# Two scan slots per tile in a selective-scan kernel: a ring of three double tiles, GpSimd's product for two slots at once, B and C loaded two slots at a time

## The chip, the cores and the metric

The kernel runs on one core of one Trainium2 chip. The metric is the device time of one execution in microseconds (us). A core has TensorE (PE, matrix products), VectorE (DVE), ScalarE (ACT), GpSimd (POOL) and SyncE (SP, which here issues every DMA), and 16 DMA engines that move data between HBM and the on-chip memory SBUF. Matrix products land in PSUM. SBUF and PSUM have 128 partitions. Every engine works through its own queue in order, and an instruction that has to wait holds all that stand behind it on its queue.

## What is computed

The input x has shape (8, 512, 48, 48): 8 samples, 512 channels, L = 2304 positions. There are two layers, each with a group norm ahead and a residual sum behind:

```python
x = x + linear_attention(group_norm(x), Wq, Wkv)       # causal, 8 heads
x = x + mamba_blocks(group_norm(x), ...)               # 4 channel groups, one after another
```

The second layer cuts the channels into four groups of 128. Each group is added to the result of the one ahead and goes through a selective scan with 256 inner channels d and 16 states n:

```python
delta = softplus(dt @ Wdt.T + bdt);  A = -exp(A_log)
dA  = exp(delta[b,l,d] * A[d,n]);    dBu = (delta * xs)[b,l,d] * Bm[b,l,n]
h   = dA_t * h + dBu_t               # for t = 0 .. L-1
y_t = sum over n of h[d,n] * C_t[n]
```

Then y is gated, projected back to 128 channels, and fused with the group's input by a maximum and two weights that depend on means over all positions.

## The kernel before, in words

**Jobs and slots.** A job is one chunk of LC = 384 positions of one channel group of one sample; NC = 6 chunks make a block, 4 blocks a sample, so there are 192 jobs. Two streams (even and odd samples) take turns, block by block. A job has SLOTS = 8 slots. In a slot, NG = 2 pairs of states are scanned for one half h of the inner channels (slots 0 to 3 have h = 0, slots 4 to 7 h = 1). The partitions carry 64 channels times the two states of a pair; a tile u holds [128, NG, 2, 1 + 384] numbers, where column 0 holds the state that the chunk ahead left.

**The work of a slot.** `last_product` (line 866) takes a tile u from its ring, lets ScalarE copy the old state into column 0 (L872), and lets GpSimd write the product of B and delta*x for the last TAIL = 128 columns (L873). `product` (L884) has VectorE write the other 256 columns, with delta*x from a copy in PSUM (`inputs`, L857). `decay` (L894) has ScalarE make exp(delta*A) in a PSUM bank; four `scan` instructions (L905, VectorE) run the recurrence over u in place; `weigh` (L917, GpSimd) multiplies u by C in place; `keep` (L928) saves the last column as the state; `gather` (L933, TensorE) sums over the states into PSUM.

**The order.** It is written out by hand in `slot(k)` and issued in that order to all engines. Slot k starts with `product` of slot k+1, then `beside(2k)`, then its four scans. After the second scan come the `gather` of slot k-2, `last_product` of slot k+2 (with s == 7 its `product` too), and `beside(2k+1)`. After the fourth scan `weigh` of slot k is issued. The ring of u has 5 buffers, so `last_product` of slot k+2 takes the buffer that slot k-3 had.

**Halves and tasks.** `beside(half)` runs what is due in this half slot: attention chunks (`chunk`, with times counted in halves), statistics, the passing on of a block's result, and the steps of `prepare` for later jobs. With first = 2*start, the half at which a job's first slot starts, `prepare` makes the convolution at first-21 to first-19, then gate, steps and delta, stores delta and dx = delta*xs (L822, GpSimd) to HBM (`spread`, L789), and from first-7 on loads them back, repeated over the two states of a pair: `steps(h)` for delta (tile dr), `scaled(h)` for dx (tile dxr), two DMAs each (L800), one for each half of the partitions.

**B and C.** `rows(m, q)` (line 810) loads the rows of B (m = 0) or C (m = 1) that the slots q and q+4 use: from the HBM tile scr, two DMAs (L813), one for each 64 partitions, each with a source of [64, 768], all 64 rows the same 3072 B. B and C have 4 buffers each, one for each q, so a job's tile q takes the buffer of the job ahead. B goes out at first-6, -5, -3 and -1, C at first-2, first, +2 and +4. `scaled(1)` goes at first+1, `steps(1)` at first+3. The order of rows in scr is set by `bc_rows` on the host.

**Start and end.** `statistics(0)` borrows five buffers of the ring of u for the first sample's chunks; the sixth chunk is loaded after the first one's statistics. At the very end `pass_on` of the second stream borrows three of them.

Of the kernel before, what the change touches and what calls it, by code (L numbers as in the profile page):

```python
# [9 lines left out]
F32 = mybir.dt.float32  # L10
# [7 lines left out]
P = 128  # L18
T = 128
LC = 384  # L20
NG = 2
SLOTS = 8
TAIL = 128
BANKS = 6
DEPTH = 3
LEAD = 11
# [23 lines left out]
def attention_then_mamba_kernel(  # L50
# [12 lines left out]
    nc = tc.nc  # L63
    B, _, L = x.shape
    NS = 16
    NC = L // LC
# [160 lines left out]
    def statistics(b):  # L227

        xv = x[b].rearrange("(t p) l -> p t l", p=P)
        stats = small.tile([P, 4, NC, 6], F32, tag="stats_a", name=f"stats_a{b}", bufs=2)  # L230
        if b == 0:

            xs = []

            def load(c):
                t = mpool.tile([P, 4, 1 + LC], F32, tag="u", name=f"xs_{c}", bufs=5)[:, :, 0:LC]
                nc.sync.dma_start(out=t, in_=xv[:, :, c * LC : (c + 1) * LC])
                xs.append(t)

            for c in range(5):  # L240
                load(c)
            load_projections()
            for c in range(NC):
                for ct in range(4):
                    nc.vector.bn_stats(stats[:, ct, c, :], xs[c][:, ct, :])
                if c == 0:
                    load(5)
                    fetch(0)
        else:
            when = begins[b] + b % 2  # L250
            for i in range(4 * NC):
                yield (when - 4, 1) if b > 1 else "1", 0
                xs = piece(b, i)
                yield (when, 1) if b > 1 else "1", 0
                nc.vector.bn_stats(stats[:, i // NC, i % NC, :], xs)
                when += PERIOD
        norms[b] = yield from group_norm(stats, 4, f"a{b}", 2)
# [266 lines left out]
    class Stream:  # L524
# [55 lines left out]
        def pass_on(self):  # L580
# [49 lines left out]
            if last and self.z:  # L630

                got = [
                    mpool.tile([P, 4, 1 + LC], F32, tag="u", name=f"end_{i}", bufs=5)
                    for i in range(NC // 2)
                ]
                for c in range(NC):
                    fu, xa = (got[c // 2][:, c % 2 * 2 + i, 0:LC] for i in range(2))
                    cols = slice(c * LC, (c + 1) * LC)
                    rows = slice(old[1] * P, (old[1] + 1) * P)
                    nc.sync.dma_start(out=xa, in_=x1s[old[0]][rows, cols])  # L640
                    nc.sync.dma_start(out=fu, in_=old[3][:, cols])
                for c in range(NC):
                    fu, xa = (got[c // 2][:, c % 2 * 2 + i, 0:LC] for i in range(2))
                    cols, icols = slice(c * LC, (c + 1) * LC), slice(3 + c * LC, 3 + (c + 1) * LC)
                    for t, i in ((xi[:, icols], 0), (fu, 1)):
                        nc.vector.scalar_tensor_tensor(
                            xa, t, wt[:, i : i + 1], xa, ALU.mult, ALU.add
                        )
                    nc.sync.dma_start(out=out[old[0], rows, cols], in_=xa)
                return  # L650
# [39 lines left out]
    class Job:  # L690
# [6 lines left out]
        def prepare(self):  # L697
# [95 lines left out]

            src = scr.rearrange("(q i m f) l -> q m i (f l)", q=4, m=2, i=2)

            def pairs(t, rows):
                for i in range(2):
# [2 lines left out]
            def steps(h):  # L802
                self.dr[h] = drs[h]
                pairs(self.dr[h][:, :, 1 : 1 + LC], dsrc[h])
# [3 lines left out]
                pairs(self.dxr[h], xsrc[h])  # L808

            def rows(m, q):  # L810
                t = mpool.tile([P, NG, LC], F32, tag="BC"[m], name=f"{'BC'[m]}_{n}_{q}", bufs=4)
                for i in range(2):
                    nc.sync.dma_start(  # L813
                        out=t[i * 64 : i * 64 + 64].rearrange("p j l -> p (j l)"),
                        in_=src[q, m, i].partition_broadcast(64),
                    )
                (self.B, self.C)[m][q] = t

            dx = mpool.tile([P, 2, LC], F32, tag="dx", name=f"dx_{n}", bufs=1)
# [10 lines left out]
            yield first - 6, 0  # L830
            rows(0, 0)
            yield first - 5, 0
            rows(0, 1)
            self.prepared = True
            yield first - 3, 0
            rows(0, 2)
            yield first - 2, 0
            rows(1, 0)
            yield first - 1, 0
            rows(0, 3)  # L840
            yield first, 0
            rows(1, 1)
            yield first + 1, 0
            scaled(1)
            yield first + 2, 0
            rows(1, 2)
            yield first + 3, 0
            steps(1)
            yield first + 4, 0
            rows(1, 3)  # L850

        prepared = closed = False

        def inputs(self, h):

# [9 lines left out]

        def last_product(self, s):

            shape, cols = [P, NG, 2, TAIL], slice(LC - TAIL, LC)
            u = mpool.tile([P, NG, 2, 1 + LC], F32, tag="u", name=f"u_{self.n}_{s}", bufs=5)
            if self.c:  # L870
                h, q = s // 4, s % 4 * NG
                nc.scalar.copy(u[:, :, :, 0], self.state[:, h, q : q + NG, :])  # L872
            nc.gpsimd.tensor_tensor(  # L873
                u[:, :, :, 1 + LC - TAIL :],
                self.B[s % 4][:, :, cols].unsqueeze(2).to_broadcast(shape),
                self.dxr[s // 4][:, :, cols].unsqueeze(1).to_broadcast(shape),
                ALU.mult,
            )
            return u

        def product(self, s, u):

            shape, cols = [P, NG, 2, LC - TAIL], slice(0, LC - TAIL)
            nc.vector.tensor_mul(  # L884
                u[:, :, :, 1 : 1 + LC - TAIL],
                self.B[s % 4][:, :, cols].unsqueeze(2).to_broadcast(shape),
                self.dxp.unsqueeze(1).to_broadcast(shape),
            )

# [25 lines left out]
        def weigh(self, s, u):  # L915

            nc.gpsimd.tensor_tensor(  # L917
                u[:, :, :, 0:LC],
                u[:, :, :, 1:],
                self.C[s % 4].unsqueeze(2).to_broadcast([P, NG, 2, LC]),  # L920
                ALU.mult,
            )

# [216 lines left out]
    def prime(k):  # L1140
        job, s = at(k)
        hurry(k, lambda: job.prepared)
        primed.add(k)
        job.inputs(0)
        for r in range(2):
            us[k + r] = job.last_product(s + r)
        job.product(s, us[k])
        ahead(DEPTH)

    def slot(k):  # L1150
        job, s = at(k)
        end = k + 1 == slots or apart(k + 1)
        if not end and k + 1 not in drawn:
            j, r = at(k + 1)
            j.product(r, us[k + 1])
        before = jobs[k // SLOTS - 1] if k >= SLOTS else None
        if s == 2 and before is not None and not before.closed:
            before.gated(1)
            tasks.insert(0, Task(finale(before)))
        elif s == 6:  # L1160
            job.gated(0)
        beside(2 * k)
        for i in range(4):
            job.scan(s, i, us[k], decays.pop(0))
            if i == 0 and s in (2, 6):
                j = at(k + 2)[0] if s == 6 and k + 2 < slots and not apart(k + 2) else None
                early = j is not None and j.prepared
                if early:
                    j.inputs(0)
                job.skip(s // 4)  # L1170
            ahead(DEPTH)
            if i == 1:

                while kept:
                    kept.pop(0)()
                if len(waiting) > 1:
                    waiting.pop(0)()
                if s == 2:
                    job.inputs(1)
                elif s == 6 and not early and k + 2 < slots and not apart(k + 2):  # L1180
                    j = at(k + 2)[0]
                    if not j.prepared:
                        hurry(k + 2, lambda: j.prepared)
                    j.inputs(0)
                if not end and k + 2 < slots and not apart(k + 2):
                    j, r = at(k + 2)
                    us[k + 2] = j.last_product(r)
                    if s == 7:

                        j.product(r, us[k + 2])  # L1190
                        drawn.add(k + 2)
                beside(2 * k + 1)
        u = us[k]
        job.weigh(s, u)
        kept.append(lambda: at(k)[0].keep(s, u))
        waiting.append(lambda: at(k)[0].gather(s, us.pop(k)))
        if end:
            close(k)
            if k + 1 < slots:
                prime(k + 1)  # L1200
            else:
                hurry(slots, lambda: not tasks)
                flush()
# [101 lines left out]
```

## Time and profile before

| | |
|---|---|
| median of 3 runs | 8292.5 us (8291.23 to 8294.32) |
| the profiled execution | 8294.55 us, span in the profile 8292.4 us |
| first scan (L905) starts, last one starts | 192.9 us, 8269.5 us |
| first B load issued | 183.2 us |
| one scan (L905), 6144 of them | 935 ns |
| GpSimd: weighing L917, product L873, 1536 each | 3191 ns, 1287 ns |
| VectorE: product L884, 1536 | 1193 ns |
| ScalarE: state copy L872, 1280; copy to PSUM L857, 384 | 194 ns, 592 ns |
| B loads, us to landing, shortest, median, longest | 3.1, 4.6, 8.0 |
| C loads, the same | 3.0, 5.2, 9.6 |

In the groups below, a line has the code line, engine, operation, tiles out<-in, shape and count; then total busy time in us and the mean of one in ns; then the engine's idle time ahead of them, and who ended it. Matrix products are pipelined, so a busy TensorE is not one at its peak. An issue of a DMA is listed with its size and the time from issue to landing. Packets are the single pieces that the DMA engines move. The DMA share in a stretch is the mean busy share of the 16 engines, by packet times.

### The profile page before, as it was taken

How to read it: one execution, taken by the hardware profiler on the slowest of the kernel's cores; microseconds unless marked ns; L12 is line 12 of the kernel's file. 1: busy time of each engine (PE TensorE's matmuls, PEld its weight loads, DVE VectorE, ACT ScalarE, POOL GpSimd, SP SyncE). 2: the span in 40 equal slices, each digit the busy share in tenths (PEclk: the TensorE clock that was granted, in tenths of full speed). 3: DMA queues.
4: the chain of work that ended last, by engine and by line, in shares of the span. 5: the costliest groups of instructions: out<-in, count | busy, mean ns of one | idle time of the engine just before them, and what ended most of it. 6: DMA issues, size and time to landing. Idle time of an engine off the chain costs nothing. (4 is left out here: it accounts for less than half of the span.)

```text
span 8292.4 us, 128570 instructions
## 1 busy us (share of the span) xinstructions
PE 7748.5 (93%) x38850; PEld 3744.1 (45%) x38850; DVE 7952.3 (96%) x10534; ACT 6911.0 (83%) x14630; POOL 7759.7 (94%) x4235
## 2 busy tenths in 40 slices
PE   8999999998999999999999999999999999999975
PEld 4444444444444444444444444444444444444432
DVE  3999999999999999999999999999999999999998
ACT  3888888887888888888888888888888888888876
POOL 2999999999999999999999999999999999999998
PEclk9999999999999999999999999999999999999987
DMA  6667777766777777777777777777777777777665
GB/s 202 190 190 204 210 206 209 208 193 197 208 204 201 201 208 209 204 205 196 201 207 201 197 205 209 208 208 193 202 200 207 201 201 197 201 200 196 191 169 145
DMA packets 974440, 1654.65 MB, mean 200 GB/s; under 512 B 119337, under 2 KB 768169, under 8 KB 973618
## 3 DMA queue, kind: packets, MB, share of 16 engines
q1 hardware_dynamic: 973746, 1646.43, 72.2%
q8 instruction: 309, 5.06, 0.3%
q14 instruction: 385, 3.15, 0.1%
HBM read 1318.28 MB, written 327.68 MB: 198 GB/s over the span
## 5 line engine op out<-in xcount | busy, mean ns | idle before, releaser
L905 DVE TENSOR_TENSOR_SCAN u<-bank,u 128x385 f32<-128x385 f32 (+1 forms) x6144 | 5439.5, 935 | 132.0 <-ACT bank L894 129.5
L917 POOL TENSOR_TENSOR u<-u,C 128x1536 f32<-128x1536 f32 x1536 | 4901.4, 3191 | 344.6 <-DVE u L905 147.3
L894 ACT ACTIVATE bank<-dr,scales 128x385 f32<-128x385 f32 (+1 forms) x6144 | 3411.6, 578 | 673.8 <-DVE u L905 639.4
L933 PE MATMUL yp<-u,cst 128*64 128x384 f32 x12288 | 2371.8, 507 | 236.2 <-ACT yp L862 160.3
L873 POOL TENSOR_TENSOR u<-B,dxr 128x512 f32<-128x512 f32 x1536 | 1977.2, 1287 | 17.3 <-DMA B<-scr 15.7
L884 DVE TENSOR_TENSOR u<-B,dxp 128x1024 f32<-128x1024 f32 x1536 | 1831.7, 1193 | 8.2 <-ACT dxp L857 8.2
L302 PE MATMUL bank<-xn,wq 128*128 128x384 f32 x4608 | 1659.1, 502 | 90.9 <-POOL xn L326 47.8
L933 PEld LDWEIGHTS yp<-u,cst 128*64 128x64 f32 x12288 | 776.5, 138 | 1412.3 <-issue 997.1
L302 PEld LDWEIGHTS bank<-xn,wq 128*128 128x128 f32 x4608 | 833.2, 191 | 838.4 <-DVE u L905 124.3
L709 PE MATMUL bank<-xi,wk 128*128 128x384 f32 x3072 | 1103.5, 502 | 9.5 <-POOL xi L683 6.3
L709 PEld LDWEIGHTS bank<-xi,wk 128*128 128x128 f32 x3072 | 556.2, 191 | 553.3 <-DVE u L905 94.0
L314 ACT ACTIVATE ex<-bank,bqkv_sb 128x384 f32<-128x384 f32 x384 | 220.3, 574 | 416.2 <-PE bank L302 416.1
L894 ACT ACT_TABLE_LOAD x382 | 490.1, 1283 | 6.7
L822 POOL TENSOR_TENSOR dx<-delta,xs 128x384 f32<-128x384 f32 x384 | 387.4, 1009 | 22.2 <-ACT delta L780 22.2
L951 PE MATMUL bank<-yz,scales 128*128 128x384 f32 x768 | 305.4, 514 | 38.4 <-DVE yz L945 30.6
L769 PE MATMUL bank<-dbc,steps_w 9*128 9x384 f32 x768 | 305.5, 517 | 3.4 <-ACT dbc L761 2.4
L720 PE MATMUL bank<-xi,scales 128*128 128x384 f32 x768 | 290.0, 492 | 2.6 <-ACT xs L745 2.1
L756 PE MATMUL bank<-xs,scales 128*40 128x384 f32 x768 | 279.5, 486 | 0.0
L857 ACT COPY dxp<-dxr 128x512 f32<-128x512 f32 x384 | 227.2, 592 | 37.0 <-DMA dxr<-xscr 19.2
L500 PE MATMUL bank<-sm,v 128*64 128x128 f32 x2304 | 253.0, 298 | 0.0
L745 ACT ACT_TABLE_LOAD x192 | 246.3, 1283 | 4.9 <-PE bank L709 1.5
L780 ACT ACT_TABLE_LOAD x192 | 246.3, 1283 | 4.0 <-issue 0.6
(118 smaller groups left out, 7907.2 us busy)
## 6 DMA issues: line engine op xcount, KB each, us to landing
B<-scr SPq DMA_DIRECT2D x1536, 192.0 KB, 4.6
C<-scr SPq DMA_DIRECT2D x1536, 192.0 KB, 5.2
xn<-xn SPq DMA_DIRECT2D x192, 768.0 KB, 7.1
dr<-dscr SPq DMA_DIRECT2D x768, 192.0 KB, 3.8
dxr<-xscr SPq DMA_DIRECT2D x768, 192.0 KB, 4.8
dscr<-delta SPq DMA_DIRECT2D x192, 384.0 KB, 6.9
xscr<-dx SPq DMA_DIRECT2D x192, 384.0 KB, 2.4
xn<-in_x SPq DMA_DIRECT2D x48, 768.0 KB, 6.6
```

What stands on the lines that cost most here:

```text
L302: nc.tensor.matmul(ps, wqs[m // NC][:, kt, j * P : (j + 1) * P], xn[:, kt, :], start=(kt == 0), stop=(kt == 3),)
L709: nc.tensor.matmul(xc, wk[:, k, h * P : (h + 1) * P], xi[:, c0 + k : c0 + k + LC], start=(k == 0), stop=(k == 3),)
L720: nc.tensor.matmul(zp, w_gate[:, s, h * P : (h + 1) * P], xi[:, c0 + 3 : c0 + 3 + LC], start=True, stop=True,)
L769: nc.tensor.matmul(vp, steps_w[32:41, s, h * P : (h + 1) * P], dbc[32:41, :], start=True, stop=True)
L822: nc.gpsimd.tensor_tensor(dx[:, h, :], delta[:, h, :], xs[:, h, :], ALU.mult)
L873: nc.gpsimd.tensor_tensor(u[:, :, :, 1 + LC - TAIL :], self.B[s % 4][:, :, cols].unsqueeze(2).to_broadcast(shape), self.dxr[s // 4][:, :, ...
L884: nc.vector.tensor_mul(u[:, :, :, 1 : 1 + LC - TAIL], self.B[s % 4][:, :, cols].unsqueeze(2).to_broadcast(shape), self.dxp.unsqueeze(1).to ...
L894: nc.scalar.activation(dA[:, cols], self.dr[h][:, g, cols], AF.Exp, scale=w_a[:, self.w[1], 2 * h + g, q + j : q + j + 1],)
L905: nc.vector.tensor_tensor_scan(u[:, j, g, cols], dA[:, cols], u[:, j, g, cols], 0.0, ALU.mult, ALU.add,)
L917: nc.gpsimd.tensor_tensor(u[:, :, :, 0:LC], u[:, :, :, 1:], self.C[s % 4].unsqueeze(2).to_broadcast([P, NG, 2, LC]), ALU.mult,)
L933: nc.tensor.matmul(self.yp[g * 64 : g * 64 + 64, 0:LC], pair_sum, u[:, j, g, 0:LC], start=False, stop=(s % 4 == 3 and j == NG - 1), skip_g ...
L951: nc.tensor.matmul(self.xm[:, 0:LC], w_out[:, self.w[1], h, :], self.yz[:, h, :], start=(h == 0), stop=(h == 1),)
```

## The change

The tile u now holds two slots: [128, 4, 2, 1 + 384], in a ring of 3 (six slots in all). `last_product` is called in even slots only, for slots k+2 and k+3 together: one copy of the old states and one GpSimd product with 4 state pairs. It hands back two views of the tile, one for each slot. TAIL goes from 128 to 144, so VectorE's product has 240 columns. B and C tiles hold two slots' rows, [128, 4, 384], with 2 buffers each; `part` picks a slot's share. A tile is loaded by one DMA whose source is [2, 64, 1536]: two rows of 6144 B in HBM, each repeated for 64 partitions. B goes out at first-6 and first-4, C at first-2 and first+3; `steps(1)` goes at first+2, ahead of the second C tile. `prepared` is set at first-5. At the start all six chunks of the first sample are loaded into the three double tiles; at the end two of them are borrowed. The host orders the rows of scr to match.

```diff
@@ -20,7 +20,7 @@
 LC = 384
 NG = 2
 SLOTS = 8
-TAIL = 128
+TAIL = 144
 BANKS = 6
 DEPTH = 3
 LEAD = 11
@@ -230,21 +230,23 @@
         stats = small.tile([P, 4, NC, 6], F32, tag="stats_a", name=f"stats_a{b}", bufs=2)
         if b == 0:
 
-            xs = []
+            xs, halves = [], []
 
             def load(c):
-                t = mpool.tile([P, 4, 1 + LC], F32, tag="u", name=f"xs_{c}", bufs=5)[:, :, 0:LC]
+                if c % 2 == 0:
+                    both = mpool.tile([P, 8, 1 + LC], F32, tag="u", name=f"xs_{c}", bufs=3)
+                    halves.append(both)
+                t = halves[c // 2][:, c % 2 * 4 : c % 2 * 4 + 4, 0:LC]
                 nc.sync.dma_start(out=t, in_=xv[:, :, c * LC : (c + 1) * LC])
                 xs.append(t)
 
-            for c in range(5):
+            for c in range(NC):
                 load(c)
             load_projections()
             for c in range(NC):
                 for ct in range(4):
                     nc.vector.bn_stats(stats[:, ct, c, :], xs[c][:, ct, :])
                 if c == 0:
-                    load(5)
                     fetch(0)
         else:
             when = begins[b] + b % 2
@@ -630,9 +632,12 @@
             if last and self.z:
 
                 got = [
-                    mpool.tile([P, 4, 1 + LC], F32, tag="u", name=f"end_{i}", bufs=5)
-                    for i in range(NC // 2)
+                    mpool.tile([P, 2 * NG, 2, 1 + LC], F32, tag="u", name=f"end_{i}", bufs=3).rearrange(
+                        "p a b l -> p (a b) l"
+                    )
+                    for i in range(2)
                 ]
+                got = [got[0][:, 0:4], got[0][:, 4:8], got[1][:, 0:4]]
                 for c in range(NC):
                     fu, xa = (got[c // 2][:, c % 2 * 2 + i, 0:LC] for i in range(2))
                     cols = slice(c * LC, (c + 1) * LC)
@@ -793,7 +798,7 @@
 
 
 
-            src = scr.rearrange("(q i m f) l -> q m i (f l)", q=4, m=2, i=2)
+            src = scr.rearrange("(q i m f) l -> q m i (f l)", q=2, m=2, i=2)
 
             def pairs(t, rows):
                 for i in range(2):
@@ -808,12 +813,11 @@
                 pairs(self.dxr[h], xsrc[h])
 
             def rows(m, q):
-                t = mpool.tile([P, NG, LC], F32, tag="BC"[m], name=f"{'BC'[m]}_{n}_{q}", bufs=4)
-                for i in range(2):
-                    nc.sync.dma_start(
-                        out=t[i * 64 : i * 64 + 64].rearrange("p j l -> p (j l)"),
-                        in_=src[q, m, i].partition_broadcast(64),
-                    )
+                t = mpool.tile([P, 2 * NG, LC], F32, tag="BC"[m], name=f"{'BC'[m]}_{n}_{q}", bufs=2)
+                nc.sync.dma_start(
+                    out=t.rearrange("p j l -> p (j l)"),
+                    in_=src[q, m].unsqueeze(1).to_broadcast([2, 64, 2 * NG * LC]),
+                )
                 (self.B, self.C)[m][q] = t
 
             dx = mpool.tile([P, 2, LC], F32, tag="dx", name=f"dx_{n}", bufs=1)
@@ -830,26 +834,22 @@
             yield first - 6, 0
             rows(0, 0)
             yield first - 5, 0
+            self.prepared = True
+            yield first - 4, 0
             rows(0, 1)
-            self.prepared = True
-            yield first - 3, 0
-            rows(0, 2)
             yield first - 2, 0
             rows(1, 0)
-            yield first - 1, 0
-            rows(0, 3)
-            yield first, 0
-            rows(1, 1)
             yield first + 1, 0
             scaled(1)
             yield first + 2, 0
-            rows(1, 2)
+            steps(1)
             yield first + 3, 0
-            steps(1)
-            yield first + 4, 0
-            rows(1, 3)
+            rows(1, 1)
 
         prepared = closed = False
+
+        def part(self, tiles, s):
+            return tiles[s % 4 // 2][:, s % 2 * NG : s % 2 * NG + NG]
 
         def inputs(self, h):
 
@@ -865,25 +865,25 @@
 
         def last_product(self, s):
 
-            shape, cols = [P, NG, 2, TAIL], slice(LC - TAIL, LC)
-            u = mpool.tile([P, NG, 2, 1 + LC], F32, tag="u", name=f"u_{self.n}_{s}", bufs=5)
+            shape, cols = [P, 2 * NG, 2, TAIL], slice(LC - TAIL, LC)
+            u = mpool.tile([P, 2 * NG, 2, 1 + LC], F32, tag="u", name=f"u_{self.n}_{s}", bufs=3)
             if self.c:
                 h, q = s // 4, s % 4 * NG
-                nc.scalar.copy(u[:, :, :, 0], self.state[:, h, q : q + NG, :])
+                nc.scalar.copy(u[:, :, :, 0], self.state[:, h, q : q + 2 * NG, :])
             nc.gpsimd.tensor_tensor(
                 u[:, :, :, 1 + LC - TAIL :],
-                self.B[s % 4][:, :, cols].unsqueeze(2).to_broadcast(shape),
+                self.B[s % 4 // 2][:, :, cols].unsqueeze(2).to_broadcast(shape),
                 self.dxr[s // 4][:, :, cols].unsqueeze(1).to_broadcast(shape),
                 ALU.mult,
             )
-            return u
+            return [u[:, 0:NG], u[:, NG : 2 * NG]]
 
         def product(self, s, u):
 
             shape, cols = [P, NG, 2, LC - TAIL], slice(0, LC - TAIL)
             nc.vector.tensor_mul(
                 u[:, :, :, 1 : 1 + LC - TAIL],
-                self.B[s % 4][:, :, cols].unsqueeze(2).to_broadcast(shape),
+                self.part(self.B, s)[:, :, cols].unsqueeze(2).to_broadcast(shape),
                 self.dxp.unsqueeze(1).to_broadcast(shape),
             )
 
@@ -917,7 +917,7 @@
             nc.gpsimd.tensor_tensor(
                 u[:, :, :, 0:LC],
                 u[:, :, :, 1:],
-                self.C[s % 4].unsqueeze(2).to_broadcast([P, NG, 2, LC]),
+                self.part(self.C, s).unsqueeze(2).to_broadcast([P, NG, 2, LC]),
                 ALU.mult,
             )
 
@@ -1142,8 +1142,7 @@
         hurry(k, lambda: job.prepared)
         primed.add(k)
         job.inputs(0)
-        for r in range(2):
-            us[k + r] = job.last_product(s + r)
+        us[k], us[k + 1] = job.last_product(s)
         job.product(s, us[k])
         ahead(DEPTH)
 
@@ -1184,7 +1183,8 @@
                     j.inputs(0)
                 if not end and k + 2 < slots and not apart(k + 2):
                     j, r = at(k + 2)
-                    us[k + 2] = j.last_product(r)
+                    if s % 2 == 0:
+                        us[k + 2], us[k + 3] = j.last_product(r)
                     if s == 7:
 
                         j.product(r, us[k + 2])
@@ -1251,10 +1251,10 @@
 
     bc_rows = [
         8 + 16 * m + 2 * (q + j) + i
-        for q in range(0, 8, NG)
+        for q in range(0, 8, 2 * NG)
         for i in range(2)
         for m in range(2)
-        for j in range(NG)
+        for j in range(2 * NG)
     ]
     win = np.swapaxes(np.asarray(L1_conv_in_proj_w), 1, 2)
     packed = [
```

## The prediction

> **What bounds the kernel now.** I read the busy line first, then busy times in the stretch from the first load of B to the last scan, then groups, waits, and last the DMA lines. The busy line shows four engines near full:
>
> ```profile
> PE 7748.5 (93%) x38850; PEld 3744.1 (45%) x38850; DVE 7952.3 (96%) x10534; ACT 6911.0 (83%) x14630; POOL 7759.7 (94%) x4235
> ```
>
> By stretch (columns: us, then busy us of PE, weight loads, DVE, ACT and POOL, clock, DMA share, GB/s):
>
> ```profile
> 8.00:12.00 4.00, 0.00 (x0) 0.00 (x0) 3.67 (x9) 0.00 (x0) 0.00 (x0) 1.00 1.07 380
> 183.00:8271.00 8088.00, 7592.20 (x37930) 3649.29 (x37930) 7888.32 (x10366) 6848.94 (x14504) 7721.53 (x4174) 0.98 0.73 200
> 3000.00:3420.00 420.00, 402.86 (x2043) 195.87 (x2044) 419.17 (x558) 365.44 (x783) 404.69 (x216) 1.00 0.78 211
> ```
>
> The reader is to see that VectorE sets the pace: 419.17 of 420 us in the middle stretch. 8088 us hold 192 jobs of 8 slots, so a job takes 42.1 us and a slot 5.27. DMA is at 73 to 80%, hidden. The groups that the change touches:
>
> ```profile
> L905 DVE TENSOR_TENSOR_SCAN u<-bank,u 128x385 f32<-128x385 f32 (+1 forms) x6144 | 5439.5, 935 | 132.0 <-ACT bank L894 129.5
> L917 POOL TENSOR_TENSOR u<-u,C 128x1536 f32<-128x1536 f32 x1536 | 4901.4, 3191 | 344.6 <-DVE u L905 147.3
> L873 POOL TENSOR_TENSOR u<-B,dxr 128x512 f32<-128x512 f32 x1536 | 1977.2, 1287 | 17.3 <-DMA B<-scr 15.7
> L884 DVE TENSOR_TENSOR u<-B,dxp 128x1024 f32<-128x1024 f32 x1536 | 1831.7, 1193 | 8.2 <-ACT dxp L857 8.2
> ```
>
> And DMA (packets; the kernel's queue; issues with KB and us to landing; SyncE's longest wait):
>
> ```profile
> DMA packets 974440, 1654.65 MB, mean 200 GB/s; under 512 B 119337, under 2 KB 768169, under 8 KB 973618
> q1 hardware_dynamic: 973746, 1646.43, 72.2%
> B<-scr SPq DMA_DIRECT2D x1536, 192.0 KB, 4.6
> C<-scr SPq DMA_DIRECT2D x1536, 192.0 KB, 5.2
> ...
> steps_w<-in_wdt SPq DMA_DIRECT2D x1, 36.0 KB
> bqkv_sb<-in_bqkv SPq DMA_DIRECT2D x1, 6.0 KB, 2.8
> ```
>
> ```profile
> SPq L789 <- POOL dx L822: 1085.2, 192, 9.1
> ```
>
> B and C are 3072 issues of 192 KB, 604 of the queue's 1646 MB. GpSimd and VectorE almost never wait for them.
>
> [...] The issue list adds up to 7451; if each leaves one small packet per engine used, 7450 x 16, plus 9 for the one transfer of 9 rows (steps_w, 36 KB), plus the 128 rows of 48 B of bqkv_sb make 119,337, which is the page's count to the unit. No issue with an outermost 2 is in this trace. [...] the stretch at 8 us, with every engine full, moves 380 GB/s, 23.75 per engine. [...] the rows of 384 and 512 elements (L822 and L873, 1009 and 1287 ns) give 2.17 too, but 512 to 1536 gives 1.86.
>
> **The change part by part.**
>
> *The 16 columns off VectorE.* L884 goes from 1024 to 960 elements. From 384 elements (L945, 547 ns) to 1024 (1193) an element costs 1.01 ns: 64 x 1.01 = 65 ns, 1536 times 99 us. VectorE is the bound now, so all would count. The copy that feeds it (L857) shrinks from 512 to 480, some 12 us of ScalarE, off the path.
>
> *GpSimd's product for two slots.* 1536 of 512 elements become 768 of 1152. With 1.86 ns, 1287 + 640 x 1.86 = 2477 against 2574 for two, 75 us less in all; with 2.17, 2676, 78 us more. I take zero. Queued behind the longer instruction is the weighing L917 of the same slot: in even slots GpSimd has 2.5 to 2.7 + 3.19 us, and mostly another 1.0, in a slot of 5.27, in odd slots only 3.19 and the rest. The weighing so comes up to 1.6 us later; its reader, the gather on TensorE, is put one and a half slots (7.9 us) after the scans, which covers 3.2 + 1.6. Without this cover TensorE would wait up to 1.6 us in each of 768 pairs.
>
> *The ring.* Before, slot k+2 takes the buffer of k-3; after, the pair k+2, k+3 takes that of k-4, k-3. The last gather waited for is the same: nothing. The state copy L872 (1280 x 194 ns) becomes 640 of 8 elements, up to 124 us less of ScalarE, which has 1239 us free in the stretch: nothing.
>
> *Start and end.* All six loads of x go at once, ahead of the weights and the first xn; the last stage uses two tiles of the ring. A microsecond either way, taken as zero.
>
> *B and C tiles of two slots.* Bytes are equal, rows double to 6144 B, issues fall from 16 to 4 a job. At 0.58 us an issue SyncE is freed of 7 us a job, and is not the bound. The loads of B's second half move from 3 to 4 halves ahead of the job, after the product that last reads the old tile; C's second half goes out 3 halves into the job, now behind both dxr and dr of h=1 (two issues each, past which it is moved), needed at the end of slot 2. With 16 engines all that would be hidden: 768 KB in 2 to 3 us of movement.
>
> But the source of the one new transfer is [2, 64, 1536], outermost 2, where the two old ones were [64, 768]. [...] it runs on **2 of 16 engines**. The price, per job and for each of these two: B and C 604 MB / 192 / 2 = 1573 KB; everything else (1646 - 604 = 1042 MB, still over 16) 339 KB. At 23.75 GB/s that is 66.2 + 14.3 = 80.5 us, against a compute time of 42.1: DMA on two engines becomes the bound. Bounds of the rate: the page's mean, 1646 MB / (72.2% x 16 x 8292.4 us) = 17.19 GB/s[...] gives 111 us[...]. I take 23.75, since 14 engines will be mostly idle.
>
> *What is late next.* Each load can go only when its tile is free. When C's second half lands, GpSimd weighs slot 2 (3.19), then makes the second half of dx (1.01), which the same queue holds behind it; SyncE stands at that store (the wait shown above), stores it (2.4) and only then asks for the next job's dr, dxr and B. 6.6 us; xn and other loads already queued fill about half: 3.3 us. The rest of the chain (two weighings, the product, VectorE's scans) lies beside the next transfers of 16.6 us each. So 83.8 us a job.
>
> *Sum.* 183 us ahead of the first B, 192 x 83.8 = 16,090, 21 us after the last scan: 16,294, and 2.1 that lie outside the span (8294.55 less 8292.4): **16,300**. The profiled run is 2 us above the median shown, 8292.5, which is nothing here. The 99 us saved on VectorE vanish: VectorE will idle half of the time.
>
> **The rivals.**
> 1. *All 16 engines carry it, faster*[...]. 8292.4 - 99 + 2 = 8195, GpSimd's 7722 up to 78 more in 7989 still fitting. For it: the same bytes in larger rows[...]. It decides once the transfer gets about 4 engines: 393 KB + 339 KB, 31 us, fits in 42.1.
> 2. *Two engines at the slow rate*: rows read 64 times over by one engine move no faster than the 17.19 GB/s mean. B and C 91.5, the rest 14.3, gap 3.3: 109 us, 21,150. For it: B and C now make up much of the mean.
> 3. *16 engines, but GpSimd binds*: 78 us dearer product and weighings in bursts; its 7800 us with the 366 idle in the stretch kept: 8166 + 204 + 2, 8370. Against: a third of that idle time is waiting for the scans of VectorE, which get earlier.
>
> **How the numbers follow.** Main case 0.74, rival 1 0.12, rival 2 0.12, rival 3 0.02. The main case's own range is 14,100[...] to 19,000; I reach up to rival 2, 21,200, and leave out the fast cases. 0.2% (17 us) is about what a measurement tells from no change. Faster 0.11, same 0.02 (rival 1 where GpSimd takes back the gain), slower 0.87.
>
> **What would show it.** Small packets: 119,337 - 3072 x 16 + 768 x 2 = 71,721 with two engines, 82,473 with sixteen. B and C landing in 16 us or more; mean near 101 GB/s; GpSimd waiting before L917 for C and before the product for B, VectorE half idle; L884 near 1128 ns, the pair product 2477 to 2676. Wrong if B and C land in under 8 us, or if the queue's rate per engine on the two is far from 23.75.

## The result, and the profile after

| | before | after |
|---|---|---|
| median, us | 8293.41 (4 runs, 8291.23 to 8298.3) | 15,896.73 (4 runs, 15,892.3 to 15,898.02) |
| ratio, 95% interval | | 1.9161 (1.9137 to 1.9185) |
| span of the profiled execution, us | 8292.4 | 15,895.2 |

The forecast was 16,300. The page after, its busy line, the packets and the kernel's queue:

```profile
PE 9627.3 (61%) x38850; PEld 4459.1 (28%) x38850; DVE 7953.6 (50%) x10534; ACT 6930.6 (44%) x13990; POOL 7850.8 (49%) x3467
...
DMA packets 828456, 1653.93 MB, mean 104 GB/s; under 512 B 71721, under 2 KB 720553, under 8 KB 827698
...
q1 hardware_dynamic: 827826, 1646.24, 31.7%
```

The reader is to see three things. The busy time of VectorE (7952 before, 7954 after) and GpSimd (7760, 7851) hardly moved, so the 7600 us are idle time. The bytes are the same. And the DMA share fell to 31.7% while the kernel waits for DMA, which fits if a few of the 16 engines are full and the rest idle. The trace's packet records, each with its start and length, bear this out: after the first load of B exactly two packets are in flight for 64% of the time, and none for 1.5%; before, 16 was the commonest number (25% of the time), and none for 20%. The small packets say the same: 71,721 is, to the unit, 119,337 less 3072 x 16 plus 768 x 2.

The groups after (columns as before) show where the time stands:

```profile
L917 POOL TENSOR_TENSOR u<-u,C 128x1536 f32<-128x1536 f32 x1536 | 4864.6, 3173 | 4922.7 <-DMA C<-scr 4666.0
L905 DVE TENSOR_TENSOR_SCAN u<-bank,u 128x385 f32<-128x385 f32 (+1 forms) x6144 | 5436.0, 938 | 471.1 <-ACT bank L894 463.6
...
L884 DVE TENSOR_TENSOR u<-B,dxp 128x960 f32<-128x960 f32 x1536 | 1747.3, 1138 | 4261.9 <-DMA B<-scr 3107.6
L873 POOL TENSOR_TENSOR u<-B,dxr 128x1152 f32<-128x1152 f32 x768 | 2017.5, 2627 | 2951.9 <-DMA B<-scr 2507.1
```

GpSimd stood 4666 us for C and 2507 us for B, VectorE 3108 us for B; before, these waits were 10.7 us for C and under 65 us for B. SyncE, which issues all DMAs, was held as well. A stretch of its timeline after (start and length in us, line, transfer):

```profile
5999.85 13.85 SPq L624 DMA_DIRECT2D xb<-x  x1
...
6025.72 8.91 SPq L805 DMA_DIRECT2D dr<-dscr  x2
6034.73 0.52 SPq L817 DMA_DIRECT2D C<-scr  x1
6035.35 0.41 SPq L279 DMA_DIRECT2D xn<-xn  x1
6035.89 8.25 SPq L357 DMA_DIRECT2D before<-ksum  x2
```

In a line with x2, two issues share the length. Before, most issues took 0.3 to 0.6 us. Here a few transfers behind a load of B or C one issue lasts up to 14 us, and everything behind it on SyncE waits: the issue that follows the first one of this view starts at 6013.76 us, when the 13.85 us are over. What makes an issue last so long wasn't shown. The chain of work that ended last (shares of the span by engine, then by line) has 70% in DMA and SyncE's queue, and C leads.

```profile
DMA 60%; PE 17%; SPq 10%; POOL 6%; issue 3%; ACT 3%; DVE 1%; POOLq 0%; ACTq 0%; DVEq 0%
DMA C<-scr 36%; DMA before<-ksum 9%; DMA dxr<-xscr 8%; PE yp L933 5%; PE bank L714 5%; POOL u L917 4%; SPq L624 3%; DMA xo<-x 3%; SPq L357 3%; DMA xb<-x 2%; SPq L805 1%; SPq L817 1%; PE bank L304 1%; PE bank L725 1%; SPq L178 1%
```

The chain of before could be followed back over only a quarter of the span. In that part DMA has 1%, and VectorE's scans lead with 4%:

```profile
PE 8%; ACT 7%; DVE 6%; DMA 1%; POOL 1%; issue 1%; SPq 1%; POOLq 0%; ACTq 0%; DVEq 0%
```

### The profile page after: what moved, and what is told of

Read it like the earlier page. It is cut to its first block, busy times and chain, and to the rows that moved or that the text cites. A ratio compares the mean times of both kernels' runs of the same rounds, so it can differ in the third digit from the quotient of the medians.

```text
span 15895.2 us, 120224 instructions
## 1 busy us (share of the span) xinstructions
PE 9627.3 (61%) x38850; PEld 4459.1 (28%) x38850; DVE 7953.6 (50%) x10534; ACT 6930.6 (44%) x13990; POOL 7850.8 (49%) x3467
## 2 busy tenths in 40 slices
DMA packets 828456, 1653.93 MB, mean 104 GB/s; under 512 B 71721, under 2 KB 720553, under 8 KB 827698
## 3 DMA queue, kind: packets, MB, share of 16 engines
q1 hardware_dynamic: 827826, 1646.24, 31.7%
## 4 chain that ended last, share of the span: by engine, by line
DMA 60%; PE 17%; SPq 10%; POOL 6%; issue 3%; ACT 3%; DVE 1%; POOLq 0%; ACTq 0%; DVEq 0%
DMA C<-scr 36%; DMA before<-ksum 9%; DMA dxr<-xscr 8%; PE yp L933 5%; PE bank L714 5%; POOL u L917 4%; SPq L624 3%; DMA xo<-x 3%; SPq L357 3%; DMA xb<-x 2%; SPq L805 1%; SPq L817 1%; PE bank L304 1%; PE bank L725 1%; SPq L178 1%
## 5 line engine op out<-in xcount | busy, mean ns | idle before, releaser
L917 POOL TENSOR_TENSOR u<-u,C 128x1536 f32<-128x1536 f32 x1536 | 4864.6, 3173 | 4922.7 <-DMA C<-scr 4666.0
L933 PE MATMUL yp<-u,cst 128*64 128x384 f32 x12288 | 2961.6, 613 | 2218.1 <-POOL u L917 1779.7
L884 DVE TENSOR_TENSOR u<-B,dxp 128x960 f32<-128x960 f32 x1536 | 1747.3, 1138 | 4261.9 <-DMA B<-scr 3107.6
L873 POOL TENSOR_TENSOR u<-B,dxr 128x1152 f32<-128x1152 f32 x768 | 2017.5, 2627 | 2951.9 <-DMA B<-scr 2507.1
L304 PE MATMUL bank<-xn,wq 128*128 128x384 f32 x4608 | 2143.3, 619 | 551.3 <-POOL xn L328 549.1
L304 PEld LDWEIGHTS bank<-xn,wq 128*128 128x128 f32 x4608 | 1062.8, 244 | 1609.2 <-POOL xn L328 596.9
L761 PE MATMUL bank<-xs,scales 128*40 128x384 f32 x768 | 529.9, 844 | 1294.1 <-DVE u L905 1294.1
L379 PE MATMUL bank<-before,cst 128*128 128x384 f32 x288 | 233.0, 913 | 1113.7 <-DMA before<-ksum 1113.7
L857 ACT COPY dxp<-dxr 128x480 f32<-128x480 f32 x384 | 217.9, 567 | 1348.6 <-DMA dxr<-xscr 1341.0
L449 PE MATMUL bank<-cst,rdb 128*128 128x128 f32 x576 | 161.0, 415 | 881.3 <-DVE u L905 880.8
L945 DVE TENSOR_TENSOR yz<-yp,sz 128x384 f32<-128x384 f32 x384 | 212.8, 554 | 660.3 <-PE yp L933 660.3
```

The lines of the kernel that those rows point to most:

```text
L304: nc.tensor.matmul(ps, wqs[m // NC][:, kt, j * P : (j + 1) * P], xn[:, kt, :], start=(kt == 0), stop=(kt == 3),)
L379: nc.tensor.matmul(kc, ident, before, start=False, stop=True)
L761: nc.tensor.matmul(dps[0:40, 0:LC], w_x[:, s, h, :], xs[:, h, :], start=(h == 0), stop=(h == 1))
L873: nc.gpsimd.tensor_tensor(u[:, :, :, 1 + LC - TAIL :], self.B[s % 4 // 2][:, :, cols].unsqueeze(2).to_broadcast(shape), self.dxr[s // 4][: ...
L884: nc.vector.tensor_mul(u[:, :, :, 1 : 1 + LC - TAIL], self.part(self.B, s)[:, :, cols].unsqueeze(2).to_broadcast(shape), self.dxp.unsqueez ...
L917: nc.gpsimd.tensor_tensor(u[:, :, :, 0:LC], u[:, :, :, 1:], self.part(self.C, s).unsqueeze(2).to_broadcast([P, NG, 2, LC]), ALU.mult,)
```

## Experiments

All times stand against the kernel before on the same chip (8295 us). "Per job" is (span - 204) / 192, with the 204 us of start and end that the prediction used. Experiments 2, 3, 5 and 8 are single executions; their differences are over 2900 us.

**1. Sixteen engines for the same tiles.** The changed kernel with:

```diff
-                nc.sync.dma_start(
-                    out=t.rearrange("p j l -> p (j l)"),
-                    in_=src[q, m].unsqueeze(1).to_broadcast([2, 64, 2 * NG * LC]),
-                )
+                for i in range(2):
+                    nc.sync.dma_start(
+                        out=t[i * 64 : i * 64 + 64].rearrange("p j l -> p (j l)"),
+                        in_=src[q, m, i].partition_broadcast(64),
+                    )
```

> The changed kernel with one edit: each double tile of B or C comes by two transfers with a source of [64, 1536] in place of one of [2, 64, 1536]. Theory (two of sixteen DMA engines carry B and C, and they are the bound): back to 16 engines, B and C hidden, 8,150 to 8,275 us, VectorE over 96% busy, small packets 119,337 - 49,152 + 1536 x 16 = 94,761. Rival (coarser tiles with two buffers are asked for too late, or the double product holds the weighing back): nothing of that is undone here, so above 12,000 us with GpSimd still waiting for B and C.

8369.8 us, ratio 1.0090 (1.0074 to 1.0107). The page shows full engines again and the small packets of the expectation:

```profile
PE 7778.3 (93%) x38850; PEld 3760.4 (45%) x38850; DVE 7878.4 (94%) x10534; ACT 6856.7 (82%) x13990; POOL 7848.4 (94%) x3467
...
DMA packets 851509, 1654.13 MB, mean 198 GB/s; under 512 B 94761, under 2 KB 743593, under 8 KB 850738
```

One edit takes away 7527 of the 7603 us. (It also makes two transfers of one; experiment 8 has two transfers a tile on two engines, and stays slow.) But the rest of the change is not the gain that was expected: 8370 lies above the kernel before and outside 8,150 to 8,275. Experiments 6 and 7 look for that.

**2. Two engines with the tiles of before.** The kernel before with its two transfers of [64, 768] made one:

```diff
-                for i in range(2):
-                    nc.sync.dma_start(
-                        out=t[i * 64 : i * 64 + 64].rearrange("p j l -> p (j l)"),
-                        in_=src[q, m, i].partition_broadcast(64),
-                    )
+                nc.sync.dma_start(
+                    out=t.rearrange("p j l -> p (j l)"),
+                    in_=src[q, m].unsqueeze(1).to_broadcast([2, 64, NG * LC]),
+                )
```

> The kernel before with one edit: each single-slot tile of B or C comes by one transfer with a source of [2, 64, 768]; tiles, ring, TAIL and load dates are those of before. Theory: the same 1573 KB a job on each of two engines, 80 to 85 us a job, so 15,000 to 16,500 us, small packets 119,337 - 49,152 + 1536 x 2 = 73,257. Rival (tile size, buffers and order are the cause): as before, 8,250 to 8,340 us.

15,787 us, small packets 73,257 as expected:

```profile
DMA packets 928339, 1654.29 MB, mean 105 GB/s; under 512 B 73257, under 2 KB 722089, under 8 KB 927538
```

That is 7492 us more than before. The slowdown needs nothing of the rest of the change: it comes with the tile size, buffers and dates of before.

**3 and 4. Four and eight engines.** The changed kernel with R = 2 or 4 copies of the rows in HBM (`scr` R times as large, one `save` into each copy; R stands for the number in the code):

```diff
-            src = scr.rearrange("(q i m f) l -> q m i (f l)", q=2, m=2, i=2)
+            src = scr.rearrange("(q i r m f) l -> q m (i r) (f l)", q=2, m=2, i=2, r=R)
...
-                    in_=src[q, m].unsqueeze(1).to_broadcast([2, 64, 2 * NG * LC]),
+                    in_=src[q, m].unsqueeze(1).to_broadcast([2 * R, 64 // R, 2 * NG * LC]),
```

> The changed kernel, with the rows of B and C stored twice in HBM so that the source of a load is [4, 32, 1536], outermost 4 in place of 2 (one more store of 48 KB a job). Theory: four engines, each 786 + 339 KB a job,[...] 45.7 to 47.4 us, a little over the 42.1 of the compute: 9,000 to 9,900 us with what of the handshake stays open. Rival (two engines whatever the dimension, or the coarser tiles): 15,000 us or more.

> As the one with outermost 4, with rows stored four times and a source of [8, 16, 1536]. Theory: eight engines, each 393 + 339 KB a job, 31 us, under the compute time of 42.1: DMA no longer binds, 8,150 to 8,400 us. Rival: 15,000 us or more; or, if bursts of 393 KB on an engine can't be hidden, 8,500 to 9,500 us with GpSimd waiting for C.

11,204 us with four and 9648.7 us (ratio 1.1632, 1.1610 to 1.1653) with eight: a clear step down with each doubling, which speaks against the rivals that put it at 15,000, but both above the theory's range. The second rival of experiment 4, 8,500 to 9,500 us with GpSimd waiting for C, comes nearest and is still 150 us too low. The packets of the two, and what GpSimd still waits for with eight engines:

```profile
DMA packets 834602, 1663.39 MB, mean 148 GB/s; under 512 B 71721, under 2 KB 726697, under 8 KB 833842
...
DMA packets 851500, 1682.30 MB, mean 174 GB/s; under 512 B 76329, under 2 KB 743593, under 8 KB 850738
...
POOL u L919 <- DMA C<-scr: 972.3, 264, 7.9
```

Both counts come out if a load leaves 4 or 8 small packets, and the store of a copy, whose outermost dimension is 4, leaves 4 where the one store of before left 16. As the stores change too, the count alone doesn't settle it; the packet records do. Packets of 6144 B are in flight two at a time for 73% of the time in the changed kernel, four at a time for 51% in experiment 3, eight at a time for 38% in experiment 4.

The term that failed in these two expectations is the time of a packet. It was taken as the same for any number of engines; the trace's packet records of 6144 B (4% of them are weights) say otherwise. In the table the last but one column is rows per job on a loaded engine times that mean, plus what the other transfers take on it. The profile doesn't tell which engine carried a packet, so this last part is the mean of all 16. The table is an account made with measured packet times, not a forecast:

| version | engines for B and C | packet, ns | on a loaded engine per job, us | measured per job, us |
|---|---|---|---|---|
| changed | 2 | 258 | 256 x 0.258 + 17.6 = 83.6 | 81.7 |
| experiment 2 (3072 B) | 2 | 130 | 512 x 0.130 + 18.0 = 84.7 | 81.2 |
| experiment 3 | 4 | 304 | 128 x 0.304 + 18.9 = 57.8 | 57.3 |
| experiment 4 | 8 | 428 | 64 x 0.428 + 20.9 = 48.4 | 49.2 |
| experiment 1 | 16 | 403 | 32 x 0.403 + 18.9 = 31.8 | 42.5 |

With 2, 4 and 8 engines the packet time of a loaded engine and the job's time agree within 5%: those engines are full nearly all the time, and with eight they are still slower than the compute. With 16 they are not full.

**5. One half of the load.** The changed kernel, C as one transfer, B as two (the lines replaced are left out):

```diff
+                if m:
                     nc.sync.dma_start(
                         out=t.rearrange("p j l -> p (j l)"),
                         in_=src[q, m].unsqueeze(1).to_broadcast([2, 64, 2 * NG * LC]),
                     )
+                for i in range(0 if m else 2):
+                    nc.sync.dma_start(
+                        out=t[i * 64 : i * 64 + 64].rearrange("p j l -> p (j l)"),
+                        in_=src[q, m, i].partition_broadcast(64),
+                    )
```

> The changed kernel, with the loads of B as two transfers of 64 partitions and those of C left as one with outermost 2. Theory (the time is the packet time of the two busiest engines): C 2 x 64 rows of 258 ns = 33.0, B's share 16 rows of 260 to 400 ns = 4.2 to 6.4, others 17.1, so 54 to 57 us a job, 10,600 to 11,100 us; small packets 119,337 - 49,152 + 768 x 16 + 384 x 2 = 83,241. Rival (each load's own lateness of some 17 us counts, not the sum on an engine): C's loads are the last to be needed and are all still late, so 13,000 us or more.

11,751 us, 60.1 a job; small packets 83,241 as expected. That is 650 us above the range, and 1250 below the rival. With packets as measured (339 ns over both kinds; C at 258 leaves 413 for B's) a loaded engine has 128 x 0.258 + 16 x 0.413 + 17.6 = 57.2 us, so some 3 us a job are not filled. The time follows the sum on the two engines in the main; the rest may be lateness of single loads, which wasn't tested.

**6. The split of the columns.** Experiment 1 with TAIL at 128 and at 136, and the kernel before with TAIL at 144:

```diff
-TAIL = 144
+TAIL = 128
```

> Two transfers per tile as in the first experiment (8370 us), and TAIL back at 128, so GpSimd's double product has 1024 elements and VectorE's 1024. Theory (GpSimd's chain set the pace at TAIL 144, VectorE's at 128): GpSimd drops by 768 x 128 x 2.1 ns = 206 us, VectorE rises by 1536 x 64 x 1.01 = 99, so VectorE binds as in the kernel before: 8,240 to 8,310 us. Rival (VectorE binds in both, and the coarse loads or bursts cost the 76 us): 8370 + 99 = 8,470 us.

> As the first of these with TAIL 136, halfway. Theory of two engines near balance: VectorE's stretch 7888 - 50 + 200 idle = 8,038, GpSimd's 7810 - 103 + 355 idle = 8,062, plus 205 outside: 8,230 to 8,290 us, the fastest of the three settings. Rival (VectorE alone binds, 99 us per 16 columns, from 8370 at 144): 8,420 us.

```diff
-TAIL = 128
+TAIL = 144
```

> The kernel before with TAIL at 144 alone: GpSimd's single-slot product of 576 elements, VectorE's of 960. Theory (GpSimd becomes the bound as soon as it takes more): 1536 x 64 x 2.1 ns = 206 us more on GpSimd, 8,420 to 8,520 us. Rival (VectorE is the only bound, as the prediction read it): 99 us less, 8,195 us.

8369.2 us (ratio 1.0090, 1.0075 to 1.0105), 8374.0 (1.0097, 1.0080 to 1.0113) and 8317.6 (1.0027, 1.0017 to 1.0037). All three miss both theories. The stretches from the first B load to the last scan (columns as in the prediction), first with two transfers per tile, at TAIL 144 (experiment 1) and at TAIL 128:

```profile
183.00:8348.20 8165.20, 7622.30 (x37959) 3666.74 (x37960) 7815.08 (x10367) 6795.28 (x13865) 7810.20 (x3406) 0.98 0.75 198
183.00:8343.90 8160.90, 7621.91 (x37921) 3656.73 (x37919) 7893.26 (x10365) 6818.43 (x13862) 7612.50 (x3405) 0.98 0.74 198
```

TAIL 128 gives VectorE 78 us more work and GpSimd 198 less, and the time is the same. So neither engine's work alone sets it here. At TAIL 128 VectorE has as much work as in the kernel before (7893 us against 7888) and GpSimd less (7612 against 7722), and yet the time is 74 us longer: the loss is in waiting. Then the kernel before, as it was and with TAIL 144:

```profile
183.00:8271.00 8088.00, 7592.20 (x37930) 3649.29 (x37930) 7888.32 (x10366) 6848.94 (x14504) 7721.53 (x4174) 0.98 0.73 200
```

```profile
183.00:8286.00 8103.00, 7587.87 (x37934) 3657.33 (x37932) 7814.36 (x10366) 6848.85 (x14505) 7922.30 (x4174) 0.98 0.72 199
```

VectorE has 74 us less work, GpSimd 201 more. GpSimd is then 97.8% busy, VectorE 96.4%, and the time rises by 22 us. Work taken from VectorE is no gain when GpSimd, itself 95.5% busy before, gets it. Whether the limit passes from VectorE to GpSimd on the way, or both hold each other up throughout, this run doesn't separate.

**7. The coarse tiles of B and C alone.** The kernel before with its ring of five, single products and TAIL 128, and only this from the change:

```diff
-                t = mpool.tile([P, NG, LC], F32, tag="BC"[m], name=f"{'BC'[m]}_{n}_{q}", bufs=4)
+                t = mpool.tile([P, 2 * NG, LC], F32, tag="BC"[m], name=f"{'BC'[m]}_{n}_{q}", bufs=2)
```

with the changed kernel's dates, `part` and row order, two transfers a tile.

> The kernel before with double tiles of B and C alone: two buffers each, loaded by two transfers of 64 partitions at the dates of the changed kernel; the ring of five single tiles, the single products and TAIL 128 stay. Theory (the coarser tiles, free later and asked for later, cost what the two-transfer versions lose whatever the TAIL): 8,340 to 8,390 us, VectorE waiting some 50 us for B. Rival (the double product and the double ring cost it): 8,280 to 8,310 us.

8340.1 us (ratio 1.0051, 1.0038 to 1.0065), at the lower edge of the theory and above the rival's range. VectorE's product now waits for B, which it did not before, and SyncE for the tile to be free:

```profile
DVE u L880 <- DMA B<-scr: 51.7, 69, 2.5
```

```profile
SPq L813 <- POOL u L913: 339.9, 347, 4.9
```

Before, SyncE's wait for the weighing at this line was 43.2 us. So 45 of the 74 us (the same with TAIL 128 as with 144, experiment 6) come with the coarse tiles. The other 30 come with the double product and the double ring, or with how these act together with the tiles; they were not taken apart further.

**8. Where the two engines write.** The changed kernel with two copies of the rows, and two transfers a tile (the lines replaced are left out):

```diff
+                for i in range(2):
+                    nc.sync.dma_start(
+                        out=t[i * 64 : i * 64 + 64].rearrange("p j l -> p (j l)"),
+                        in_=src[q, m, i].unsqueeze(1).to_broadcast([2, 32, 2 * NG * LC]),
+                    )
```

> The changed kernel with each row of B and C stored twice in HBM and each double tile loaded by two transfers of [2, 32, 1536], so that two engines carry it as before, but both write into the same half of the partitions at a time, at the same place in their 32. Theory (packets lengthen where two engines write to partitions of one group at a time, as may be behind the 304 and 428 ns of the versions with four and eight engines): packets of some 470 ns, 256 a job on each engine, 120 + 18 us a job, 24,000 to 28,500 us. Rival (packets lengthen for another reason, such as reads of HBM): 258 to 300 ns, 15,800 to 18,300 us.

16,435 us, 84.5 us a job: the rival's case. With two engines that write in one half of the partitions a packet took 266 ns, with a half for each 258. The trace doesn't tell whether they were at the same place in their 32 at the same time, and with 8 and 16 engines each has fewer partitions than 32, so the run doesn't rule out such a meeting there. It does show that two transfers in place of one are no cure as long as each runs on two engines.

Within experiments 3 and 4 packets of 6144 B are longer where more packets are in flight: 268 ns on average with about four and 427 with about 17 in experiment 3, 366 with about eight and 532 with about 17 in experiment 4. In the changed kernel they take only 292 with about 15 in flight, so the number isn't the whole of it. What lengthens them stays open.

## Why the prediction was right, point by point

- **Two of 16 engines.** Right to the unit in the small packets, and the cause: undone alone it gives back 7527 of 7603 us (experiment 1), done alone it gives 7492 us (experiment 2). That an outermost dimension of 2 means two engines was not shown ahead of the result: the small packets of before fit 16 engines for a transfer, and 9 for the one of 9 rows. The runs now show it for 2 by the count (71,721 and 73,257) and the packets in flight, and for 4 and 8 by the count together with the packets in flight (experiments 3 and 4).
- **The rate of an engine.** 23.75 GB/s was taken. The rows of B and C took 258 ns for 6144 B, 23.8 GB/s: 66.0 us where the sum had 66.2.
- **All other transfers.** 14.3 us were taken, at the full rate; their packets (most of 1536 B) took 17.6, as a mean over the 16 engines.
- **The gap while SyncE stands at the store of dx.** 3.3 us were taken. No packet at all is in flight for 1.5% of the time, 1.2 us a job, so little of this gap is left. The packets of a loaded engine then add up to 66.0 + 17.6 = 83.6 us, 2 us more than the 81.7 of a job: records overlap a little, or the two engines have less than the mean of the other transfers. That the sum of 83.8 came within 2.5% is in part luck: the 3.3 us of gap that weren't there stood in for the 3.3 us that the other transfers took longer.
- **What would show it.** GpSimd waits before L917 for C and before the product for B, VectorE is busy half of the time, mean 104 GB/s against 101, L884 1138 ns against 1128, the pair product 2627 against 2477 to 2676. The landing times that were named can't be read: the profile gives none for these transfers after.

Steps that failed, though they don't show in this result:

- **"VectorE is the bound now, so all would count."** They did not. The 419 of 420 us of one stretch were read as VectorE setting the pace; GpSimd's 404.7 in the same row leave only 15.3. Moving 16 columns cost 22 us in the kernel before where 99 were to be gained (experiment 6).
- **GpSimd's product at zero.** One of 1152 elements takes 2639 ns in experiment 1, two of 512 take 2574, 50 us more in all. GpSimd's busy time there is 7848 against 7760, 89 us more where zero was taken and 78 was the upper bound. The rest of it is overlap: GpSimd's instructions overlap at their ends, so that their lengths add up to 203 us more than its busy time before, and to only 139 in experiment 1, which has fewer of them. On the time this had no visible effect (experiment 6).
- **"With 16 engines all that would be hidden."** The double tiles cost 45 us by themselves (experiment 7): SyncE waits longer for them to come free, and VectorE then for B. So rival 1, at 8195, was wrong by 175 us: with sixteen engines the change is still 0.9% slower. Rival 3, GpSimd binding at 8370, has the number of experiment 1 (8369.8), but by luck: with 198 us less work for GpSimd the time stays (experiment 6).
- **"It decides once the transfer gets about 4 engines."** Four give 11,204, eight 9649. The sum under it had the wrong number of engines: 393 KB of B and C are the share of one engine in eight, and with four it is 786 KB, which with the other 339 KB makes 47.4 us at 23.75 GB/s, over the 42.1 of the compute. The expectation of experiment 3 has it right. Even eight were not enough (49.2 us a job where 31 were reckoned), as the packet time was not the constant that it was taken for.

## What to carry to other kernels

Before two transfers are merged, look at the outermost dimension of the new source: with a 2 there, one transfer in place of two turned a hidden load of 604 MB into the bound and nearly doubled the kernel's time, at the same bytes, longer rows and fewer issues. The mean DMA share was low here, 31.7%, while two engines were full nearly all the time; count the small packets per transfer (in these runs the counts fit one for each engine used), and work out the load of the fullest engine. And where two engines are both above 95% busy, as VectorE and GpSimd here, cost both before work is moved from one to the other, and by the time from start to start where instructions overlap (GpSimd's add up to 203 us more than its busy time before).

## What was not expected of the hardware

- In the changed kernel the issue of a DMA on SyncE lasted much longer: that of xb (L624) 13.5 us in the median and up to 20.7 (before, at L622, 0.58 and 2.0). Transfers that stand behind it in the issuing order are late as well: the one behind the 13.85 us of xb above started 13.91 us after it.
- A packet of 6144 B took 258, 304, 428 and 403 ns with 2, 4, 8 and 16 engines carrying B and C; one of 3072 B took 130 with 2 (experiment 2) and 191 with 16 (before). Why is open (experiment 8).
- The granted TensorE clock was lower in the longer runs: 0.98 before (TensorE 93% busy), 0.93 with eight engines (9643 us), 0.88 with four (11,204 us), 0.76 in the changed kernel (15,897 us, TensorE 61% busy), with the gather's matrix product at 613 ns instead of 507. Experiment 1 brings the clock back to 0.98. In the changed kernel TensorE has 17% of the chain that ended last; what the lower clock costs by itself was not measured.
